# A state-space and mixture-of-experts layer: the last chunk's conv taps behind the softplus's first steps on VectorE, and eps as the bias of the square root

## The chip, the cores and the metric

The kernel runs on one core of a Trainium2 chip. The metric is the device time of the launch in microseconds (us), the median of several runs. The core's engines are named as in the profile: PE is TensorE (matrix multiply) and PEld its weight loads, DVE is VectorE, ACT is ScalarE, POOL is GpSimd, SP is SyncE, which here only issues DMAs. [...]

## The reference

The input is a sequence of 4096 tokens with 256 features. Two layers follow, each with a residual and a layer norm without weights:

```python
xz = input_tensor @ W_in                                  # 256 -> 2 x 512
conv_in, gated = xz[..., :512], xz[..., 512:]
convolved = silu(causal depthwise conv of conv_in, 4 taps, + conv_b)
x_dbl = convolved @ W_x                                   # 512 -> 33
delta = softplus(x_dbl[..., :1]); Bm, Cm = x_dbl[..., 1:17], x_dbl[..., 17:]
h = exp(delta * A) * h + delta * Bm * convolved[..., :16] # scan over the tokens, 16 states
skip_out = sum(h * Cm) + convolved * D_param
x = layernorm(x + (skip_out * silu(gated)) @ W_out)
expert = argmax(x @ Wr.T + br)                            # one of 8 experts for each token
x = layernorm(x + relu(x @ W1[expert] + b1) @ W2[expert] + b2)
```

The layer norm is `(x - m) / sqrt(v + eps)` with eps 1e-5. All is in float32.

## The kernel before, in words

The first layer works through eight blocks of 512 tokens (`TB`), the loop `for k in range(NB)` at L1018. It is pipelined by software: iteration k projects block k, works on the state space of block a = k - 1, on gate, output projection and layer norm of block b = k - 2, and on the routing of block c = k - 3. The second layer runs over 32 blocks of 128 tokens that share an expert (and up to seven that occur seldom, inside `tc.If`, L656); its quarters (`expert()`) are mixed into the last two iterations and fill the time after the loop.

`project(k, c)` (L707) takes one of eight chunks of 128 of the 1024 projected features. Its matmuls are L722. Chunks 0 to 3 are the conv's: ACT copies the result into `xc` (L729) and writes `acc`, the result times the last tap plus the bias (L731); DVE adds the three other taps, each a `scalar_tensor_tensor` over 128x512 (L735). Each tap reads and writes `acc`, so the three are a chain. ACT's silu of chunk c - 2 (L742) is issued in the call of chunk c, behind that chunk's eviction. Chunks 4 to 7 are the gate's: ACT evicts them with a silu (L727). The tiles `acc` have three buffers, the matmul banks `mm` three, the small banks `tr` two.

`gauge(a)` (L750) multiplies the convolved block by `W_x`, and ACT copies the result, `pxs`. `gauge_out(a)` (L764) transposes it (L770); ACT copies it into `parts` (L779); DVE adds the two parts into `xd` (L780). Then comes the softplus of 128x4 values as a series: DVE makes `e` (L785), ACT its exp (L786), DVE ten small steps (L792 to L801), `delta` (L803) and the two writes of `sr` (L804, L807). Meanwhile ACT puts another part into `sr` (L781). `look(k)` multiplies the block by the router's weights, ACT copies that into `rx` (L869), and `look_out(a)` transposes it (`pf`, L876), with `rparts` (L882) behind it. `scan(a)` transposes `sr` (`pt`, L816), takes an exp on ACT (L818), and scans on DVE (L820 to L830) to `hC`. `gate(b)` spreads `hC` by matmul (`py`, L842) and multiplies (L849, L854). `project_out(b, j)` is the output projection (L890) with residual and statistics (L894 to L899); for the last j it takes the square root: DVE adds eps (L904), ACT takes the root (L905), DVE the reciprocal (L906).

The experts' blocks: `hidden` (L581, relu on ACT L590 and on DVE L592), `close` (L606), `finish` with the residual (L629, L631) and the helper `layernorm` (L250): statistics (L254, L256), eps (L258), root (L259), reciprocal (L260), and the row (L261). `scatter` (L645) writes the rows out.

What sets the order: only PE's order is the program's (`tc.manual_schedule(engines={PE})`, L121). The queues of DVE, ACT, POOL and SP are ordered at build time by the framework's scheduler, which takes, of what is ready by its own estimate, what stands first in the program. `tc.issue_after` adds single edges. So `project(k, 3)`, which stands ahead of `gauge_out(a)`, has the higher rank. The part of the loop that the change touches:

Of the kernel before, what the change touches and what calls it, by code (L numbers as in the profile page):

```python
# [37 lines left out]
F32 = mybir.dt.float32  # L38
# [3 lines left out]
AF = mybir.ActivationFunctionType  # L42
ALU = mybir.AluOpType
# [4 lines left out]
P = 128  # L48
T, D = 4096, 256
DI, NS, KC = 512, 16, 4  # L50
NE, FF = 8, 1024
TB = 512
# [4 lines left out]
CC = DI // P  # L57
# [25 lines left out]
EPS = 1e-5  # L83
# [17 lines left out]
def mamba_moe(  # L101
# [17 lines left out]
    nc = tc.nc  # L119

    ctx.enter_context(tc.manual_schedule(engines={mybir.EngineType.PE}))  # L121
    const = ctx.enter_context(tc.tile_pool(name="const", bufs=1))
# [6 lines left out]
    def bank(tag, name, bufs=None):  # L129
        return ps.tile([P, 512], F32, tag=tag, name=name, bufs=bufs)  # L130
# [5 lines left out]
    st = {}  # L136

    def load(i):

        xTb = a2.tile([P, DC, TB], F32, tag="xTb", name=f"xTb{i}")  # L140
        at = slice(i * TB, (i + 1) * TB)
        if i:
            nc.sync.dma_start(xTb, xT[:, at].rearrange("(c p) t -> p c t", p=P))

        xb = a2.tile([P, JT, D + NE], F32, tag="xb", name=f"xb{i}")
        st[i] = {"xTb": xTb, "xb": xb}

    def load_rows(i):
        nc.sync.dma_start(
            st[i]["xb"][:, :, 0:D], x[i * TB : (i + 1) * TB, :].rearrange("(j p) d -> p j d", p=P)  # L150
        )
# [14 lines left out]
    cw = const.tile([P, CC, KC], F32, name="cw")  # L166
# [17 lines left out]
    def load_later():  # L184

        nc.sync.dma_start(wx[:, :, 0:XW], W_x.rearrange("(c p) n -> p c n", p=P))
        nc.sync.dma_start(al, A_log)
        nc.sync.dma_start(dp, D_param)
        nc.sync.dma_start(woutT, W_outT.rearrange("(c p) n -> p c n", p=P))
        nc.sync.dma_start(wout[:, :, 0:D], W_out.rearrange("(c p) d -> p c d", p=P))  # L190
        nc.sync.dma_start(brb, br.to_broadcast([P, NE]))
        nc.sync.dma_start(x1d[T : T + 1, :], lists[0:1, 0:D])

    ident = const.tile([P, P], F32, name="ident")
    make_identity(nc, ident)
    ones = const.tile([P, P], F32, name="ones")
# [53 lines left out]
    def layernorm(pool, rows, done, name):  # L250

        n = rows.shape[0]
        st = pool.tile([P, 6], F32, tag="st", name=f"st{name}")[0:n, :]
        nc.vector.bn_stats(st, rows)  # L254
        mv = pool.tile([P, 2], F32, tag="mv", name=f"mv{name}")[0:n, :]
        nc.vector.bn_aggr(mv, st)  # L256
        sd = pool.tile([P, 1], F32, tag="sd", name=f"sd{name}")[0:n, :]
        nc.vector.tensor_scalar(sd, mv[:, 1:2], EPS, None, ALU.add)  # L258
        nc.scalar.activation(sd, sd, AF.Sqrt)  # L259
        nc.vector.reciprocal(sd, sd)  # L260
        nc.vector.tensor_scalar(done, rows, mv[:, 0:1], sd, ALU.subtract, ALU.mult)  # L261

# [438 lines left out]
    def expert(n=1):  # L701
        for _ in range(n):
            next(quarters)

    def project(i, c):  # L707

        s = st[i]
        xTb = s["xTb"]  # L710
        if c == 0:
            if i == 0:
                s["xc"] = a2.tile([P, CC, KC - 1 + TB], F32, tag="xc", name="xc0")
                nc.gpsimd.memset(s["xc"][:, :, 0 : KC - 1], 0.0)
            s["cv"] = a3.tile([P, CC, TB], F32, tag="cv", name=f"cv{i}")
            s["sg"] = a3.tile([P, CC, TB], F32, tag="sg", name=f"sg{i}")
        xc, cv, sg = s["xc"], s["cv"], s["sg"]
        pm = bank("mm", f"pm{i}_{c}")

        for at in (slice(0, first), slice(first, TB)) if i == c == 0 else (slice(0, TB),):  # L720
            for dc in range(DC):
                nc.tensor.matmul(  # L722
                    pm[:, at], lhsT=win[:, dc, c * P : (c + 1) * P], rhs=xTb[:, dc, at],
                    start=(dc == 0), stop=(dc == DC - 1),
                )
        if c >= CC:
            evicted = nc.scalar.activation(sg[:, c - CC, :], pm, AF.Silu)  # L727
        else:
            nc.scalar.copy(xc[:, c, KC - 1 :], pm)  # L729
            acc = a3.tile([P, TB], F32, tag="acc", name=f"acc{i}_{c}")  # L730
            evicted = nc.scalar.activation(  # L731
                acc, pm, AF.Identity, scale=cw[:, c, KC - 1 : KC], bias=cb[:, c : c + 1]
            )
            for k in range(KC - 1):
                nc.vector.scalar_tensor_tensor(  # L735
                    acc, xc[:, c, k : k + TB], cw[:, c, k : k + 1], acc, ALU.mult, ALU.add
                )
            s["acc", c] = acc
        if ("acc", c - 2) in s:

            with tc.issue_after(evicted.ins):
                nc.scalar.activation(cv[:, c - 2, :], s["acc", c - 2], AF.Silu)  # L742
        if c == CC and i + 1 < NB:

            after = st[i + 1]["xc"] = a2.tile(
                [P, CC, KC - 1 + TB], F32, tag="xc", name=f"xc{i + 1}"
            )
            nc.gpsimd.tensor_copy(after[:, :, 0 : KC - 1], xc[:, :, TB : TB + KC - 1])
# [137 lines left out]
    def project_out(i, j):  # L886
        s_, sg, xb = st[i], st[i]["sg"], st[i]["xb"]
        po = bank("o", f"po{i}_{j}")
        for c in range(CC):
            nc.tensor.matmul(  # L890
                po[:, 0 : D + NE], lhsT=sg[:, c, j * P : (j + 1) * P], rhs=wout[:, c, :],
                start=(c == 0), stop=(c == CC - 1),
            )
        nc.vector.tensor_tensor(xb[:, j, :], po[:, 0 : D + NE], xb[:, j, :], ALU.add)  # L894
        if j == 0:
            s_["mv"] = a2.tile([P, JT, 2], F32, tag="mva", name=f"mva{i}")
        sta = a2.tile([P, 6], F32, tag="sta", name=f"sta{i}_{j}")
        nc.vector.bn_stats(sta, xb[:, j, 0:D])
        nc.vector.bn_aggr(s_["mv"][:, j, :], sta)  # L899
        if j < JT - 1:  # L900
            return
        mv = s_["mv"]
        sd = s_["sd"] = a2.tile([P, JT], F32, tag="sda", name=f"sda{i}")
        nc.vector.tensor_scalar(sd, mv[:, :, 1], EPS, None, ALU.add)  # L904
        nc.scalar.activation(sd, sd, AF.Sqrt)  # L905
        nc.vector.reciprocal(sd, sd)  # L906
        nm = a2.tile([P, JT], F32, tag="nma", name=f"nma{i}")
        nc.vector.scalar_tensor_tensor(nm, mv[:, :, 0], -1.0, sd, ALU.mult, ALU.mult)
        x1 = a2.tile([P, JT, D], F32, tag="x1", name=f"x1{i}", bufs=1)
        for j in range(JT):  # L910
            nc.scalar.activation(
                x1[:, j, :], xb[:, j, 0:D], AF.Identity,
                scale=sd[:, j : j + 1], bias=nm[:, j : j + 1],
            )
        nc.sync.dma_start(
            x1d[i * TB : (i + 1) * TB, :].rearrange("(j p) d -> p j d", p=P), x1
        )
# [94 lines left out]
    def have(i):  # L1012
        return 0 <= i < NB
# [4 lines left out]
    for k in range(NB):  # L1018
        if have(k + 1):
            load(k + 1)  # L1020
        if k == 0:
            load_later()
            load_rows(0)
        if have(k + 1):
            load_rows(k + 1)
        a, b, c = k - 1, k - 2, k - 3

        fill = {NB - 2: (0, 0, 0, 0, 0, 0, 2, 2), NB - 1: (1, 1, 2, 1, 1, 1, 1, 1)}.get(k, (0,) * 8)
        project(k, 0)
        if k == 2:  # L1030
            router_behind(1)
        if have(b):
            gate(b)
        expert(fill[0])
        project(k, 1)
        if have(a):
            gauge(a)
        expert(fill[1])
        project(k, 2)
        if k == 0:  # L1040
            router_weights()
        if have(c - 1):
            tokens_of(c - 1)
        expert(fill[2])
        project(k, 3)
        if have(a):
            gauge_out(a)
        if have(b):
            project_out(b, 0)
        expert(fill[3])  # L1050
        project(k, 4)
        if k == 1:
            router_behind(0)
        if have(c):
            rank(c)
        if have(b):
            project_out(b, 1)
        expert(fill[4])
        project(k, 5)
        if have(c):  # L1060
            blocks_of(c)
        look(k)
        if have(b):
            project_out(b, 2)
        expert(fill[5])
        project(k, 6)
        if have(a):
            look_out(a)
            scan(a)
        if k == NB - 2:  # L1070

            turn(0)
        if have(b):
            project_out(b, 3)
            choose(b)
        expert(fill[6])
        project(k, 7)
        if have(c):
            place(c)
        expert(fill[7])  # L1080
    a, b, c = NB - 1, NB - 2, NB - 3
# [99 lines left out]
```

## Time and profile before

| | |
|---|---|
| time, median of 3 runs | 494.23 us (493.94 to 494.93) |
| profiled execution | 493.76 us, its span 492.1 us |
| granted TensorE clock | 0.991 |
| PE busy | 472.7 us, 96% |
| DVE busy | 346.9 us, 71% |
| ACT busy | 218.8 us, 44% |
| POOL busy | 187.3 us, 38% |
| conv taps, L735 | 96, 71.2 us, mean 771 ns |
| eps adds, L258 and L904 | 32 of 150 ns, 5 of about 142 ns and 8 of 170 ns |
| roots, L259 and L905 | 45, 202 to 206 ns |

A profile line of a group reads: line, engine, operation, out<-in by the program's names, shapes, count, then busy time, mean duration and the idle time of the engine ahead of it with what ended that. A timeline line has start and duration in us, and in brackets the idle time ahead of it. Ends of matmuls are modelled. A part of the time, 1.66 us, lies outside the span. The rows of digits cut the span into 40 slices, each the busy share in tenths.

By stretches of the span: from 50 to 290 us (the loop and what follows of the first layer) PE is busy 237.58 of 240 us and DVE 210.52; from 290 to 440 us PE 149.60 of 150 and DVE 86.45; from 440 us to the end PE 38.52 of 52 and DVE 20.33.

### The profile page before, as it was taken

How to read it: one execution, taken by the hardware profiler on the slowest of the kernel's cores; microseconds unless marked ns; L12 is line 12 of the kernel's file. 1: busy time of each engine (PE TensorE's matmuls, PEld its weight loads, DVE VectorE, ACT ScalarE, POOL GpSimd, SP SyncE). 2: the span in 40 equal slices, each digit the busy share in tenths (PEclk: the TensorE clock that was granted, in tenths of full speed). 3: DMA queues.
4: the chain of work that ended last, by engine and by line, in shares of the span. 5: the costliest groups of instructions: out<-in, count | busy, mean ns of one | idle time of the engine just before them, and what ended most of it. 6: DMA issues, size and time to landing. Idle time of an engine off the chain costs nothing. (4 is left out here: it accounts for less than half of the span.)

```text
span 492.1 us, 7641 instructions
## 1 busy us (share of the span) xinstructions
PE 472.7 (96%) x2602; PEld 353.0 (72%) x2602; DVE 346.9 (71%) x1161; ACT 218.8 (44%) x452; POOL 187.3 (38%) x193
## 2 busy tenths in 40 slices
PE   8999999999999999999999999999999999998893
PEld 5344645555464675777889998999989898987782
DVE  2587979797999889869899788545565655453352
ACT  4786778777878774845342221221212121211120
POOL 2002122444447345233415242444444466542433
PEclk9999999999999999999999999999999999998997
DMA  8401012120308908506666587999871599486500
GB/s 235 156 1 44 0 44 85 45 85 1 128 1 349 361 18 277 191 2 224 218 259 254 214 296 263 375 346 367 325 300 50 202 321 318 143 293 254 194 17 23
DMA packets 23052, 89.59 MB, mean 182 GB/s; under 512 B 4898, under 2 KB 14629, under 8 KB 19298
## 3 DMA queue, kind: packets, MB, share of 16 engines
q0 software_dynamic: 8672, 74.29, 41.3%
q1 hardware_dynamic: 13378, 14.50, 9.1%
q8 instruction: 23, 0.38, 0.3%
q10 hardware_dynamic: 960, 0.27, 0.3%
q14 instruction: 19, 0.16, 0.1%
HBM read 87.35 MB, written 9.54 MB: 197 GB/s over the span
## 5 line engine op out<-in xcount | busy, mean ns | idle before, releaser
L722 PE MATMUL pm<-xTb,win 128*128 128x512 f32 (+1 forms) x260 | 120.6, 595 | 0.5 <-DMA win<-in_W_in 0.5
L581 PEld LDWEIGHTS ph<-xgT,we 128*128 128x128 f32 x864 | 102.2, 194 | 9.7 <-DVEq L656 2.7
L581 PE MATMUL ph<-xgT,we 128*128 128x128 f32 x864 | 104.9, 279 | 3.3 <-DMA out<-long,tidx 2.3
L606 PE MATMUL pe<-we,hT 128*128 128x256 f32 x432 | 99.9, 381 | 0.7 <-DVE hT L592 0.7
L606 PEld LDWEIGHTS pe<-we,hT 128*128 128x128 f32 x432 | 79.5, 190 | 11.7 <-DVE hT L592 1.5
L735 DVE SCALAR_TENSOR_TENSOR acc<-xc,cw,acc 128x512 f32<-128x512 f32 x96 | 71.2, 771 | 15.5 <-ACT acc L731 15.1
L722 PEld LDWEIGHTS pm<-xTb,win 128*128 128x128 f32 x260 | 47.3, 191 | 46.9 <-issue 40.4
L520 POOL DMA_INDIRECT we<-in_experts,widx x32 | 33.8, 1056 | 95.6 <-DVE r L631 32.3
L259 ACT ACTIVATE sdm<-sdm 128x1 f32<-128x1 f32 x32 | 6.5, 202 | 132.8 <-DVE sdm L258 132.7
L890 PE MATMUL po<-wout,sg 128*128 128x264 f32 x256 | 64.1, 392 | 0.0
L854 POOL TENSOR_TENSOR sg<-cv,sg 128x512 f32<-128x512 f32 x22 | 33.9, 1543 | 59.2 <-DVE cv L849 44.3
L890 PEld LDWEIGHTS po<-wout,sg 128*128 128x128 f32 x256 | 46.0, 190 | 10.2 <-issue 2.9
L592 DVE TENSOR_SCALAR hT<-ph,we 128x128 f32<-128x128 f32 x108 | 31.5, 343 | 29.4 <-issue 9.7
L645 POOL DMA_INDIRECT out<-y,tidx x32 | 32.9, 1028 | 42.2 <-DVE y L261 30.0
L503 POOL DMA_INDIRECT xg<-x1d,tidx x32 | 32.3, 1010 | 31.7 <-issue 6.6
L631 DVE TENSOR_TENSOR r<-pe,xs 128x256 f32<-128x256 f32 x32 | 13.5, 422 | 42.3 <-PE pe L606 38.5
L590 ACT ACTIVATE hT<-ph,we 128x128 f32<-128x128 f32 x108 | 30.8, 366 | 26.5 <-PE ph L581 18.3
L979 POOL TENSOR_SCALAR rowh<-lrow,row,code 128x256 f16<-128x256 bf16 x20 | 25.8, 1299 | 26.8 <-DVE row L971 26.8
L849 DVE SCALAR_TENSOR_TENSOR cv<-cv,dp,py 128x256 f32<-128x256 f32 x64 | 28.9, 470 | 2.4 <-PE py L842 2.4
L727 ACT ACTIVATE sg<-pm 128x512 f32<-128x512 f32 x32 | 19.0, 595 | 17.1 <-PE pm L722 14.8
L581 PE MATMUL ph<-wide,we 128*128 128x160 f32 (+1 forms) x160 | 24.4, 310 | 2.3 <-DVEq L656 2.3
L581 PEld LDWEIGHTS ph<-wide,we 128*128 128x128 f32 x160 | 23.8, 190 | 2.9 <-DVEq L656 2.7
(221 smaller groups left out, 612.3 us busy)
## 6 DMA issues: line engine op xcount, KB each, us to landing
xb<-in_x SPq DMA_DIRECT2D x8, 512.0 KB, 4.8
x1d<-x SPq DMA_DIRECT2D x8, 512.0 KB, 5.4
xTb<-in_xT SPq DMA_DIRECT2D x7, 512.0 KB, 3.5
win<-in_W_in SPq DMA_DIRECT2D x1, 512.0 KB
we<-in_W_outT SPq DMA_DIRECT2D x1, 512.0 KB
wout<-in_W_out SPq DMA_DIRECT2D x1, 512.0 KB
we<-in_experts,widx POOLq DMA_INDIRECT x32
xg<-x1d,tidx POOLq DMA_INDIRECT x32
```

The source lines that it names most:

```text
L503: nc.gpsimd.indirect_dma_start(out=to, out_offset=None, in_=x1d[0:rows, :], in_offset=bass.IndirectOffsetOnAxis(ap=at, axis=0),)
L520: nc.gpsimd.indirect_dma_start(out=wes[n][:, :], out_offset=None, in_=experts, in_offset=bass.IndirectOffsetOnAxis(ap=weights[n], axis=0), ...
L581: nc.tensor.matmul(ph[:, n * w : (n + 1) * w], lhsT=we[:, at : at + P], rhs=xgT[:, dc * w : (dc + 1) * w], start=(dc == 0), stop=(dc == DC ...
L590: nc.scalar.activation(hT[:, fc, :], ph[:, n * w : (n + 1) * w], AF.Relu, bias=bias)
L592: last[b] = nc.vector.tensor_scalar(hT[:, fc, :], ph[:, n * w : (n + 1) * w], bias, 0.0, ALU.add, ALU.max)
L606: nc.tensor.matmul(py[:, 0:D], lhsT=hT[:, fc, 0:P], rhs=out_weights(fc), start=(fc == 0), stop=(fc == FC - 1),)
L645: moved = nc.gpsimd.indirect_dma_start(out=out, out_offset=bass.IndirectOffsetOnAxis(ap=at, axis=0), in_=rows, in_offset=None, bounds_chec ...
L722: nc.tensor.matmul(pm[:, at], lhsT=win[:, dc, c * P : (c + 1) * P], rhs=xTb[:, dc, at], start=(dc == 0), stop=(dc == DC - 1),)
L735: nc.vector.scalar_tensor_tensor(acc, xc[:, c, k : k + TB], cw[:, c, k : k + 1], acc, ALU.mult, ALU.add)
L849: nc.vector.scalar_tensor_tensor(cv[:, c, at], cv[:, c, at], dp[:, c : c + 1], py[:, 0 : TB // 2], ALU.mult, ALU.add,)
L854: eng.tensor_tensor(sg[:, c, :], cv[:, c, :], sg[:, c, :], ALU.mult)
L890: nc.tensor.matmul(po[:, 0 : D + NE], lhsT=sg[:, c, j * P : (j + 1) * P], rhs=wout[:, c, :], start=(c == 0), stop=(c == CC - 1),)
```

## The change

The three taps of a chunk become a helper `taps(i, c)`. `project` calls it for chunks 0 to 2 as before. For chunk 3 the loop calls it after `gauge_out(a)` and before `project_out(b, 0)`. So the sum of the gauge's parts (L780) and the softplus's steps now have the higher rank on DVE, and the last chunk's taps the lower. The adds of eps on DVE are gone at both places; a 128x1 tile with eps, set once on POOL, is the bias of ACT's square root, which now reads the variance itself. The number of taps and roots is the same.

```diff
+    eps = const.tile([P, 1], F32, name="eps")
+    nc.gpsimd.memset(eps, EPS)
     ident = const.tile([P, P], F32, name="ident")
...
-        nc.vector.tensor_scalar(sd, mv[:, 1:2], EPS, None, ALU.add)
-        nc.scalar.activation(sd, sd, AF.Sqrt)
+        nc.scalar.activation(sd, mv[:, 1:2], AF.Sqrt, bias=eps[0:n, :])
...
+    def taps(i, c):
+        acc, xc = st[i]["acc", c], st[i]["xc"]
+        for k in range(KC - 1):
+            nc.vector.scalar_tensor_tensor(
+                acc, xc[:, c, k : k + TB], cw[:, c, k : k + 1], acc, ALU.mult, ALU.add
+            )
...
-            for k in range(KC - 1):
-                nc.vector.scalar_tensor_tensor(
-                    acc, xc[:, c, k : k + TB], cw[:, c, k : k + 1], acc, ALU.mult, ALU.add
-                )
             s["acc", c] = acc
+            if c < CC - 1:
+                taps(i, c)
...
-        nc.vector.tensor_scalar(sd, mv[:, :, 1], EPS, None, ALU.add)
-        nc.scalar.activation(sd, sd, AF.Sqrt)
+        nc.scalar.activation(sd, mv[:, :, 1], AF.Sqrt, bias=eps)
...
         project(k, 3)
         if have(a):
             gauge_out(a)
+
+        taps(k, CC - 1)
         if have(b):
             project_out(b, 0)
```

## The prediction

> **What bounds the kernel now.** I read the first two parts of the page, then TensorE's own waits, then the timeline around the longest of them, then the timeline of the end.
>
> ```profile
> span 492.1 us, 7641 instructions
> PE 472.7 (96%) x2602; PEld 353.0 (72%) x2602; DVE 346.9 (71%) x1161; ACT 218.8 (44%) x452; POOL 187.3 (38%) x193
> PE   8999999999999999999999999999999999998893
> DVE  2587979797999889869899788545565655453352
> ```
>
> TensorE (PE) is the wall: it is thin only at the start and in the last tenth. VectorE (DVE) is nearly full in the chunk phase, up to about 290 us, and half idle later. So an edit on DVE or ScalarE (ACT) pays only where PE waits for it. Those places, from PE's waits:
>
> ```profile
> PE ph L581 <- DMA out<-long,tidx: 2.3, 1, 2.3
> PE ph L581 <- DVEq L656: 2.3, 1, 2.3
> ...
> PE pt L816 <- DVE mva L899: 1.4, 2, 0.7
> ...
> PE pt L816 <- ACT rx L869: 0.7, 1, 0.7
> PE ph L581 <- DVE y L261: 0.6, 1, 0.6
> ```
>
> The columns are total us, times, longest. Two families: `pt` (L816), the transposes of `sr`, which `gauge_out` ends with (L807), and `ph` (L581), the first expert matmul behind an If (L656). One `pt` wait, iteration k = 3, on the timeline:
>
> ```profile
> 79.47 4.05 DVE L735 SCALAR_TENSOR_TENSOR acc<-xc,cw,acc 128x512 f32<-128x512 f32 x6
> ...
> 81.44 0.36 ACT L779 COPY parts<-pxo 128x264 f32<-128x264 f32 x1
> ...
> 83.44 0.28 DVE L780 TENSOR_TENSOR xd<-parts 128x132 f32<-128x132 f32 x1
> 83.65 0.74 DVE L735 SCALAR_TENSOR_TENSOR acc<-xc,cw,acc 128x512 f32<-128x512 f32 x1
> ...
> 85.32 0.21 ACT L786 ACTIVATE e<-e 128x4 f32<-128x4 f32 x1
> ...
> 89.18 0.38 PE L876 MATMUL pf<-ident,rx 128*128 128x128 f32 x2
> ...
> 89.77 0.34 DVE L807 TENSOR_TENSOR sr<-xd,sr 128x64 f32<-128x64 f32 x1
> ...
> 90.26 0.61 PE L816 MATMUL pt<-ident,sr 128*80 128x128 f32 x4 [0.70 <-DVE mva L899]
> ```
>
> `parts` is there at 81.80, but `xd` starts at 83.44, because taps of chunks 2 and 3 go first; everything to `sr` (90.11) hangs on it. The page names L899, but in k = 3, 4 and 5 `pt` starts exactly 0.147 us after L807 ends, so L807 is the releaser. Start to start the transposes of a group are 0.109 us apart, and in k = 2, where nothing is late, `pt` follows `pf` by 0.109 too. With that yardstick PE loses 0.83 (k = 1), 0.86 (k = 3), 0.86 (k = 4) and 0.31 (k = 5): **2.86 us**. (The listed idle, 0.66 + 0.70 + 0.70 + 0.15, is shorter as it counts from a modelled end.) In k = 1 the last to come is not `sr` (37.48) but ACT's `rx` copy (37.79), which stands behind the exp and its table loads in ACT's queue. In k = 6 and 7 and behind the loop `sr` is early.
>
> The end, one If at 445 us:
>
> ```profile
> 443.80 0.18 DVE L256 BATCH_NORM_AGGREGATE mvm<-stm 128x2 f32<-128x6 f32 x1
> 444.01 0.15 DVE L258 TENSOR_SCALAR sdm<-mvm 128x1 f32<-128x1 f32 x1
> 444.20 0.20 ACT L259 ACTIVATE sdm<-sdm 128x1 f32<-128x1 f32 x1 [5.30 <-DVE sdm L258]
> ```
>
> PE is idle during this chain and restarts when DVE has passed the If.
>
> [...] loads last 1283 ns, and L731, with two pointers, takes 783 ns where the copy of the same tile (L729) takes 580, so about 102 each. [...] here exp stands between silus and pays a load each way (84.02 and 85.54 in k = 3). [...]
>
> **The change part by part.** The order in which PE works is written by hand; the other queues are ordered by the framework, with program order as rank, so an instruction of lower rank slips into a gap of a chain of higher rank.
>
> *Taps of chunk 3 moved behind `gauge_out`.* Nothing is added: three L735 (0.68 us apart back to back, 0.74 alone) change places in each of 8 iterations. They go past `gauge_out`'s DVE work (L780 to L807) and its ACT steps L779, L781, L786; no DMA, SP or POOL work is passed. As long as the taps of two chunks are in the queue they fill each other's gaps, and `xd` comes only at the last tap. With chunk 3 ranked behind, `xd` can go as soon as `parts` is there and a chunk 2 tap has ended: about 82.2 in k = 3 instead of 83.44, and more in k = 4, where 107.75 stands against 110.94. So `e` and the exp come 1.2 us or more earlier. From the end of `xd` to that of the exp, with its load, it is 1.8 us (83.72 to 85.53), and the chunk 3 taps (2.0 us) fill just this time, which other DVE work fills now (84.46 to 86.15). That other work then falls among the twelve small steps L792 to L807. DVE is 10.66 of 10.90 us busy from 79.4 to 90.3, so `sr` comes earlier only by what now stands in front of it and then stands behind. At least L894 and L898 at 88.96 and 89.44, which need a late matmul, should be: about 0.7 us. If more of the second projection's work falls behind, up to 1.7. Needed is 0.86. I take 0.70 each in k = 3 and 4, all 0.31 in k = 5 (its `xd` now waits from 135.23 to 138.41), and in k = 1, where the exp and with it `rx` come 0.8 earlier, 0.60 of 0.83. Sum 0.70 + 0.70 + 0.31 + 0.60 = **2.3 us**; bounds 0 and 2.86. What is late next is `py` (L842), which waits for `hC`; its chain starts from L894 of the last projection, which follows PE itself, so it moves along. DVE idles 2.32 us at 90.4, so work pushed behind `sr` has room.
>
> *The silu of chunk 3* waits for these taps: their last ends at 84.39, the silu starts at 87.33 (2.9 us of cover), then `rx` (87.85 to 88.21) has 0.8 us to `pf`. Costed at nothing; without that cover each us is a us of PE per iteration.
>
> *Sqrt with eps as bias.* 37 L258 and 8 L904 go, about 0.15 us each, 6.7 us of DVE time; each sqrt gets a pointer, 0.2 to about 0.3 us. In a waiting chain 0.19 (444.01 to 444.20) goes and 0.1 comes: 0.09 saved. It counts where PE or the end waits: the Ifs at 445, 457 and 469 us and the last block (485.34 to the end), 4 x 0.09 = **0.37 us**. Bounds: 0 if the bias fetch eats it all, 0.76 if it is free. Elsewhere ACT waits for this add (133 us listed) but nobody waits for ACT. Behind the sqrt in ACT's queue stand the next block's relus, 0.1 later at worst, and all of PE's waits for `hT` are 0.7 us.
>
> *eps memset*: one 128x1 memset on POOL ahead of the identity, 0.1 us by the constants' rows. PE's warm-up shifts, but its first real matmul waits 0.47 us for the DMA at 4.91. Nothing; 0.1 if that cover were gone.
>
> Sum: 2.3 + 0.37 = 2.7 us; I take 0.2 off because all queues are ordered anew and small waits (0.3 us at 172, 175 and 234) can grow. The profiled execution took 493.76 (span 492.1 and 1.66 around it), which gives 491.3; the median of the runs is 494.23, 0.47 higher, which gives **491.7**.
>
> **The rivals.** *Nothing at PE*: all DVE work in front of `sr` stays in front, as small work fills every gap of the twelve steps, and only the end's 0.37 is left: 493.8. For it: DVE's saturation up to 90.3. Against: L894 and L898 can't come before their matmul, and `sr` now stands behind them.
>
> *Slower*: the chunk 3 taps fall behind the softplus chain, and their silu blocks ACT in front of `rx`. It decides from a last tap later than about 88.1 (84.39 + 2.9 + 0.8). If the taps followed `sr`, they would end near 89.6, 1.5 us too late in each of k = 1 to 5: +7.5 - 2.5 = +5, so 499.2. Against: the taps still outrank the projection's and the rank work, and the exp's 1.8 us is free for them.
>
> **How the numbers follow.** Forecast 0.60, nothing 0.27, slower 0.13. A measurement of this kernel tells about 0.2% (0.99 us) from no change. A few of the second case end below 493.24: faster 0.62, same 0.25, slower 0.13. The range runs from 490.9 (2.86 + 0.5) to 494.9 (the second case with 0.7 us of new waits); it leaves out the slower case and little else.
>
> **What would show it.** Right: `xd` within 1 us of `parts` in k = 3 to 5, L786 a us earlier relative to L779, the `pt` waits gone or under 0.2, the sqrts near 295 ns, the span down by about 2.5 before 180 us and 0.3 behind 440. Wrong: `pt` still waiting on L807, a silu of chunk 3 with idle time in front of it on ACT, or a new PE wait at `py` or `pf` that takes the place.

## The result, and the profile after

| | before | after |
|---|---|---|
| median, first comparison (7 runs each) | 494.23 us | 490.78 us |
| ratio, 95% interval | | 0.9919 [0.9898, 0.994] |
| second comparison (67 and 22 runs) | 495.77 us | 493.80 us, 0.9966 [0.9949, 0.9984] |
| third comparison (34 and 18 runs) | 493.52 us | 491.32 us, 0.9957 [0.9936, 0.9978] |
| profiled execution, its span | 493.76, 492.1 us | 490.78, 489.1 us |

Faster, as forecast, and the first measured time, 490.78 us, lies 0.12 us below the range's low end of 490.9. The two later comparisons give 1.7 and 2.1 us (494 us times 0.0034 and 0.0043), less than the 2.5 us forecast. Both have to be explained: what the change itself is worth, and what the first comparison had on top.

The page of the kernel after: its head, the busy line and two rows of tenths.

```profile
span 489.1 us, 7602 instructions
PE 472.0 (97%) x2602; PEld 353.9 (72%) x2602; DVE 340.1 (70%) x1116; ACT 224.1 (46%) x453; POOL 185.2 (38%) x194
PE   8999999999999999999999999999999999998893
DVE  2587969798999988869889788545555555453352
```

DVE lost 45 instructions and 6.8 us (346.9 to 340.1). ACT gained 5.3 us: 45 roots by about 0.1 us are 4.2, and there is one more table load (49 in place of 48, 1.28 us each). As forecast, neither of these is the gain. PE's own waits after (total us, times, longest):

```profile
PE pt L822 <- ACT rx L875: 0.7, 1, 0.7
...
PE prx L869 <- DVE rk L969: 0.4, 1, 0.4
```

The two `pt` waits put down to `mva` are gone. The one of k = 1 is as it was. A new one has come: `prx`, the router's matmul, waits for `rk`. Iteration k = 3 on the timeline after:

```profile
81.00 0.38 ACT L785 COPY parts<-pxo 128x264 f32<-128x264 f32 x1
...
82.74 0.28 DVE L786 TENSOR_TENSOR xd<-parts 128x132 f32<-128x132 f32 x1
82.95 0.73 DVE L711 SCALAR_TENSOR_TENSOR acc<-xc,cw,acc 128x512 f32<-128x512 f32 x1
...
83.70 0.62 ACT L748 ACTIVATE cv<-acc 128x512 f32<-128x512 f32 x1
...
84.34 1.28 ACT L792 ACT_TABLE_LOAD   x1
...
85.63 0.20 ACT L792 ACTIVATE e<-e 128x4 f32<-128x4 f32 x1
...
85.87 0.17 DVE L798 TENSOR_SCALAR s<-e 128x4 f32<-128x4 f32 x1
...
89.57 0.24 DVE L813 TENSOR_TENSOR sr<-xd,sr 128x64 f32<-128x64 f32 x1
...
89.96 0.61 PE L822 MATMUL pt<-ident,sr 128*80 128x128 f32 x4
```

`xd` starts 1.36 us after `parts` ends (1.64 before), and all three taps of chunk 3 stand behind it, where it was one. At this place the kernel after runs 0.47 us later (a DMA at the start), so `xd` is at 82.27 on the clock of before: 82.2 was forecast. `sr` ends at 89.81 and `pt` starts with no bracket: the wait is gone.

The way there is not the same in every iteration. In k = 3 the exp (85.63, on the clock of before 85.16) comes only 0.16 us earlier than the 85.32 of before, because a silu stands ahead of its table load on ACT. The gain comes behind it: `s` (L798) starts 0.03 us after the exp has ended, where other work on DVE held it up for 0.62 us before:

```profile
84.02 1.28 ACT L786 ACT_TABLE_LOAD   x1
...
86.15 0.15 DVE L792 TENSOR_SCALAR s<-e 128x4 f32<-128x4 f32 x1
```

So `sr` ends 0.77 us earlier. In k = 4 it goes as forecast. First before, then after, which is 0.31 us ahead at this place:

```profile
107.37 0.38 ACT L779 COPY parts<-pxo 128x264 f32<-128x264 f32 x1
...
110.94 0.28 DVE L780 TENSOR_TENSOR xd<-parts 128x132 f32<-128x132 f32 x1
...
112.81 0.21 ACT L786 ACTIVATE e<-e 128x4 f32<-128x4 f32 x1
```

```profile
107.07 0.38 ACT L785 COPY parts<-pxo 128x264 f32<-128x264 f32 x1
...
108.64 0.28 DVE L786 TENSOR_TENSOR xd<-parts 128x132 f32<-128x132 f32 x1
...
111.02 0.20 ACT L792 ACTIVATE e<-e 128x4 f32<-128x4 f32 x1
```

With the 0.31 us taken off, the exp is 1.5 us earlier and `sr` 1.3 us (117.60 before, 116.03 after).

**A sum over all pairs of matmuls.** PE's 2602 matmuls have the same order in every kernel here. For each neighbouring pair I took the time from start to start in each of thirteen profiles, and what it is above the shortest of them. A wait that all thirteen have, such as that of `pt` in k = 1, doesn't show in this. Added up by place, in us (before in two executions, after in three):

| place | before | before again | after | after again | after, third |
|---|---|---|---|---|---|
| `pt`, k = 3 | 0.81 | 0.80 | 0.03 | 0.02 | 0.00 |
| `pt`, k = 4 | 0.86 | 0.86 | 0.00 | 0.00 | 0.00 |
| `pt`, k = 5 | 0.31 | 0.30 | 0.00 | 0.00 | 0.00 |
| `prx`, k = 5 | 0.02 | 0.02 | 0.48 | 0.48 | 0.49 |
| `ph` at 297 us | 0.29 | 0.28 | 0.00 | 0.00 | 0.00 |
| `ph` behind the Ifs, 443 and 455 us | 0.20 | 0.20 | 0.07 | 0.07 | 0.07 |
| **what follows the kernel** | **2.49** | **2.46** | **0.58** | **0.57** | **0.56** |
| start, up to 12 us | 1.29 | 1.59 | 1.72 | 3.77 | 1.86 |
| `po` behind a stretched `oh`, k = 4 to 6 | 0.0 | 0.0 | 0.0 | 1.73 | 0.78 |
| `pe` waiting for `hT`, 412 and 472 us | 1.27 | 1.29 | 0.00 | 1.25 | 0.00 |
| half clock, 440 to 452 us | 1.66 | 1.66 | 1.66 | 1.66 | 0.04 |

The upper part is the same to 0.03 us in every execution of a kernel: **1.9 us is the change's own** at these places. The lower part changes between executions of the same program; its rows add up to 2.7 to 8.4 us. In the two first profiles it was 1.27 (`hT`) in favour of after and 0.43 (start) against. Small waits at 171 to 174 us are in neither part: 0.70 twice before, 0.40, 0.57 and 0.57 after.

Two things remain open. A stretched `oh` (a small step of DVE, see the last section) was seen ahead of `po` in two of the three profiles of after and in none of the two of before. It meets POOL's product at the same point in both kernels (0.60 us into it), but with so few profiles it isn't shown that the change leaves this row alone. And the granted clock was higher for after: its mean was 0.9930 beside 0.9920 in the second comparison and 0.9936 beside 0.9914 in the third. One stretch of half clock is 1.66 us of time and 0.0034 of that mean. My estimate from these numbers is that at equal clock the mean times (2.1 and 2.5 us apart) differ by 1.6 and 1.4 us, a little under the 1.9.

### The profile page after: what moved, and what is told of

The parts are those of the page before. It is cut to its first block, busy times and chain, and to the rows that moved or that the text cites. A ratio compares the mean times of both kernels' runs of the same rounds, so it can differ in the third digit from the quotient of the medians.

```text
span 489.1 us, 7602 instructions
## 1 busy us (share of the span) xinstructions
PE 472.0 (97%) x2602; PEld 353.9 (72%) x2602; DVE 340.1 (70%) x1116; ACT 224.1 (46%) x453; POOL 185.2 (38%) x194
## 5 line engine op out<-in xcount | busy, mean ns | idle before, releaser
L711 DVE SCALAR_TENSOR_TENSOR acc<-xc,cw,acc 128x512 f32<-128x512 f32 x96 | 72.7, 777 | 16.0 <-ACT acc L739 15.6
L260 ACT ACTIVATE sdm<-mvm,eps 128x1 f32<-128x1 f32 x32 | 9.4, 295 | 144.2 <-DVE mvm L258 138.4
L860 POOL TENSOR_TENSOR sg<-cv,sg 128x512 f32<-128x512 f32 x22 | 32.8, 1495 | 59.4 <-DVE cv L855 45.9
L737 ACT COPY xc<-pm 128x512 f32<-128x512 f32 x32 | 18.6, 581 | 18.1 <-PE pm L730 17.8
```

The source lines that it names most:

```text
L711: nc.vector.scalar_tensor_tensor(acc, xc[:, c, k : k + TB], cw[:, c, k : k + 1], acc, ALU.mult, ALU.add)
L860: eng.tensor_tensor(sg[:, c, :], cv[:, c, :], sg[:, c, :], ALU.mult)
```

## Experiments

Each kernel computes the whole reference. Ratios are against the kernel before on the same chip: the first four ran on one chip, the next four on another, the last three on a third. The edits of the first two are shown against the kernel before, the later ones against the kernel after.

**The taps alone** (the diff's `taps`, without the bias).

```diff
             s["acc", c] = acc
+            if c < CC - 1:
+                taps(i, c)
...
+        taps(k, CC - 1)
```

> Only the three taps of chunk 3 are moved behind the gauge; the adds of eps on VectorE and the roots are as before. Theory (the gain is the pt waits of the loop): pt waits of k = 3, 4 and 5 are gone (1.9 to 2.0 us by starts of matmuls), the one of k = 1 stays at 0.83, and a new wait of about 0.45 us at prx in k = 5 comes, as rank's first step stands further back on VectorE: net 1.5 us faster than before, about 492.7. Rival (half of the gain is the shorter layer norm of the experts): at most 1.0 us faster than before, and the rest comes with the eps edit alone.

Measured: 493.80 us, 0.9969 [0.9948, 0.9989], so 1.5 us. The `pt` waits of k = 4 and 5 are gone, that of k = 3 is 0.17 in the sum, `prx` has its 0.48, `pt` of k = 1 is unchanged. By the sum: 0.64 + 0.86 + 0.31 - 0.46 = 1.35. The interval of the time, 0.5 to 2.6 us, leaves room for the rival's 1.0; it is the sum that puts the gain at these places. Its profile also had two stretched `oh`, 1.72 us.

**The bias alone** (the same at L904, and the tile `eps` as in the change).

```diff
-        nc.vector.tensor_scalar(sd, mv[:, 1:2], EPS, None, ALU.add)
-        nc.scalar.activation(sd, sd, AF.Sqrt)
+        nc.scalar.activation(sd, mv[:, 1:2], AF.Sqrt, bias=eps[0:n, :])
```

> Only the adds of eps are gone and eps is the bias of the root; the taps stand where they stood. Theory: the layer norm chain of an expert block is 0.09 us shorter, of which 0.07 are lost again where VectorE's aggregate now waits for ScalarE's reading of the variance: 0.1 to 0.2 us at the Ifs and the end in all. By the build's order of the queues the k = 3 iteration also gets another order (chunk 3's taps further back), so the pt wait of k = 3 may shrink by up to 0.8 us and that of k = 4 stays at 0.86: 0.2 to 1.0 us faster, about 493.6. Rival: the edit frees VectorE in the expert phase and takes away the waits of the hidden matmuls' evictions at 414 and 475 us (1.06 us) that the profile of before had: 1.5 us faster or more.

Measured: 494.68 us, 0.9992 [0.9969, 1.0016]. By the time alone this is no change. By the sum of pairs it has the 0.29 at 297 us and 0.13 behind the Ifs, which the taps alone have not; and `pt` of k = 3 fell to 0.29 because DVE's queue was ordered anew there; those of k = 4 and 5 stayed (0.84, 0.31). Its profile also had the stretched `oh` in three iterations, 2.7 us, which no part of the edit asks for.

**The kernel before, again.**

> The kernel before, unchanged, for a second profile. Theory: the waits of pe for hT at 414 and 475 us (0.55 and 0.51 us by starts) belong to that one execution, in which TensorE's semaphore updates came late and in bunches; they are not at these places in this profile, and the pt waits of k = 1, 3, 4 and 5 are all there with the same sizes. Rival: they belong to the program, and are at 414 and 475 us again. Time within 0.1% of the runs of before.

Measured: 496.17 us, 1.0008 [0.9988, 1.0027]. All four `pt` waits are back, and both `hT` waits at the same places in the program. So the `hT` waits are no accident of one execution, as I had thought; the later groups show that they are no part of the program either.

**The kernel after, again.**

> The changed kernel, unchanged, for a second profile on this chip. Theory: no pt wait in k = 3 to 5, pt of k = 1 at 0.83 us and prx of k = 5 at about 0.45 us again; late bunches of TensorE's semaphore updates may come at other places. Time 3 to 3.5 us below before (0.7%).

Measured: 493.80 us, 0.9966 [0.9949, 0.9984]. So 1.7 us, not the 3 to 3.5 expected. The `pt` waits are gone as in the first profile; `hT` (1.25) and two stretched `oh` (1.73) are there, which the first did not have. The profiled execution took 496.02 us against 490.78 for the same program, and its rows of the lower part add up to 8.4 us against 3.4.

**The taps behind `rank`.**

```diff
-        taps(k, CC - 1)
         if have(b):
             project_out(b, 0)
...
         if have(c):
             rank(c)
+        taps(k, CC - 1)
```

> The changed kernel with the last chunk's taps called two places later in the loop, behind rank(c). Theory (rank's rk was pushed behind the moved taps on DVE, and it frees the bank that prx needs in k = 5): rk is early again, the prx wait of 0.41 us in k = 5 is gone, the pt waits of k = 3 to 5 stay gone, and the silu of chunk 3 still has its cover; by the trace 0.4 us less than the changed kernel, ratio to before 0.995 to 0.997. Rival (the prx wait belongs to the bank's other user, or to the softplus chain that now runs at the same time): it stays at 0.3 to 0.5 us. Second rival (the taps come too late for their silu): ACT idles in front of the silu of chunk 3 in k = 3 to 5, rx is late, and pf or pt waits 0.3 us or more.

Measured: 492.01 us, 0.994 [0.9918, 0.9962]. First `rk` (DVE) and `prx` (PE) of k = 5 in the kernel after, then in this one:

```profile
139.08 0.15 DVE L969 TENSOR_TENSOR rk<-pr,oh 128x32 f32<-128x32 f32 x1
...
139.28 0.64 PE L869 MATMUL prx<-xTb,wr 128*32 128x256 f32 x8 [0.41 <-DVE rk L969]
```

```profile
136.67 0.17 DVE L969 TENSOR_TENSOR rk<-pr,oh 128x32 f32<-128x32 f32 x1
...
138.86 0.64 PE L869 MATMUL prx<-xTb,wr 128*32 128x256 f32 x8
```

`rk` comes 2.4 us earlier and the bracket is gone: the theory holds. The matmul banks `tr` are two, taken in turn, and in k = 5 a table's `pn` (at 138.70 us in after) takes the one between, so that `prx` gets the bank of `pr`, which `rk` frees. In return the taps fall among the softplus steps, and `pt` waits 0.26 in k = 4 and 0.14 in k = 3: a gain of 0.48 at one place and 0.37 back.

**`rx` of k = 1 on DVE.**

```diff
-        nc.scalar.copy(st[i]["rx"], prx[:, 0:n])
+        (nc.vector.tensor_copy if i == 1 else nc.scalar.copy)(st[i]["rx"], prx[:, 0:n])
```

> The changed kernel with the copy rx of iteration 1 alone on DVE and not on ACT. Theory (in k = 1 pt waits for ACT's rx, which stands behind the exp and its two table loads in ACT's queue, and not for sr): the pt wait of k = 1, 0.67 to 0.83 us in every profile so far, falls under 0.3, and the span loses about 0.5 us; whatever is left of the wait is sr. Rival (sr is as late as rx, or DVE reaches rx later than ACT did): the wait stays above 0.5. Nothing else moves; ratio to before 0.995 to 0.997.

Measured: 491.56 us, 0.9928 [0.9902, 0.9953]. In its profile, end of the softplus on DVE and then PE:

```profile
38.18 0.23 DVE L813 TENSOR_TENSOR sr<-xd,sr 128x64 f32<-128x64 f32 x1
...
38.55 0.60 PE L822 MATMUL pt<-ident,sr 128*80 128x128 f32 x4 [0.89 <-DVE sr L813]
```

`pt` doesn't read this `rx`: it takes the bank of `prx`, which the copy frees. The expected gain did not come. With `rx` out of ACT's queue the wait grew by 0.23, because the copy stood in front of the softplus on DVE and `sr` came at 38.41, not 37.95. In the kernel after `sr` ends 0.3 us before `rx` (37.95 and 38.26), so even an `rx` that cost DVE nothing would win no more than about that. Whether it would is not shown, as this edit moved `sr` too. The later waits for `py` (0.46 in the sum) went, so the net is a gain of 0.24.

**The taps later still**, behind `project_out(b, 1)`: a test of the slower rival.

```diff
         if have(b):
             project_out(b, 1)
+        taps(k, CC - 1)
```

> The changed kernel with the last chunk's taps called behind project_out(b, 1). It tests the slower rival of the prediction: the silu of chunk 3 stands in front of rx in ACT's queue, so taps that end more than about 3.7 us later than before hold up rx, and pf and pt with it. Theory (the cover is as costed, and here the last tap falls behind the first softplus steps): ACT idles 1 to 2 us in front of the silu of chunk 3 in k = 3 to 5, and PE waits 0.3 to 1.5 us in each of them at pf, pt or prx; 1 to 4 us slower than the changed kernel, ratio to before 0.998 to 1.005. Rival (the cover is larger than the timeline showed, or pt waits for sr in any case): no new wait of PE above 0.3 in k = 3 to 5, ratio as the changed kernel's.

Measured: 492.37 us, 0.9932 [0.9901, 0.9963], no slower than the kernel after in its comparisons, where 0.998 to 1.005 was expected. Iteration k = 4: ACT, then DVE and PE.

```profile
115.45 0.36 ACT L875 COPY rx<-prx 128x256 f32<-128x256 f32 x1
116.39 0.63 ACT L748 ACTIVATE cv<-acc 128x512 f32<-128x512 f32 x1 [0.58 <-DVE acc L711]
...
118.81 0.61 PE L822 MATMUL pt<-ident,sr 128*80 128x128 f32 x4 [0.16 <-DVE sr L813]
```

The taps do come late for their silu, which waits 0.58 us, but `rx` now runs ahead of it: the scheduler orders ACT's queue too, and put the late silu behind `rx`. So the mechanism that my slower rival named did not act here; it needs `rx` to stand behind the silu. What PE waits for is `sr` (0.33 and 0.40 in k = 4 and 3), as taps stand among the softplus steps. The price of moving too far is that, 0.8 us with k = 5, of which 0.48 comes back as `rk` is early; not 5.

**The gate's first product on DVE.**

```diff
-            eng = nc.vector if c == CC - 1 or (c % 2 and i >= NB - 2) else nc.gpsimd
+            eng = nc.vector if c in (0, CC - 1) or (c % 2 and i >= NB - 2) else nc.gpsimd
```

> The changed kernel with the gate's product of chunk 0 on DVE and not on POOL (7 or 8 instructions change the engine). In some executions the one-hot oh on DVE takes 1.2 to 1.3 us in place of 0.18 when it runs beside POOL's product, the last product is then late and PE waits 0.95 us at po. Theory (it is the meeting with POOL's first product that stretches oh): with no POOL product at that time every oh takes under 0.25 us, the po waits of 0.9 us don't occur, and the cost is about 0.6 us of DVE time for each product, which may show as a pt wait or none. Rival (oh is stretched by something else, or the next product on POOL takes the place): some oh are still above 1 us. In time 0.993 to 0.999 of before.

Measured: 494.94 us, 0.9995 [0.998, 1.001]. Every `oh` ahead of the `po` of k = 4 to 6 is at 0.18 us. That fits the theory, but three such in one profile could be chance; stronger is that in the other profiles each of the nine stretched ones ends 0.05 us behind POOL's product. And `oh` of k = 3 now meets a product and took 0.78 us. The rival's second half came true: in k = 4 to 6 the small step `earlier` (L947, 0.15 us where it is free) took 0.95 us beside the product that POOL now does first. `po` waits 0.88 in k = 4 and 5, 0.57 in k = 3, 0.71 in k = 6. All that the change had gained is gone.

**The kernel after, a third time.**

> The changed kernel a third time, on another occasion. Theory (the change's own part is about 1.9 us: 0.79, 0.86 and 0.31 at pt, less 0.46 at prx in k = 5, plus 0.29 at 297 us and 0.1 at the Ifs; what the first comparison showed above this belongs to executions, with waits for hT and half clock after pauses): ratio 0.995 to 0.9975 of before, and the profile has the same waits at pt, prx and the Ifs as the first, whatever its clock does. Rival (the first comparison's 0.992 is the change's value, and something in the other session took half of it): ratio 0.990 to 0.994.

Measured: 491.32 us, 0.9957 [0.9936, 0.9978], in the theory's range; about 1 us of it is the clock, by the estimate above. The last column of the table above is its profile: the same upper part, no `hT` waits, one stretched `oh`, full clock at 440 us.

**Rank first, `rx` on DVE, four buffers for `mv`.**

```diff
-        mv = pool.tile([P, 2], F32, tag="mv", name=f"mv{name}")[0:n, :]
+        mv = pool.tile([P, 2], F32, tag="mv", name=f"mv{name}", bufs=4)[0:n, :]
```

(with the two edits above)

> The changed kernel with the taps behind rank(c), rx of iteration 1 on DVE, and four buffers for the statistics mv of layernorm. Theory (each step takes away its own wait): no prx wait in k = 5, the py waits of k = 1 gone and pt there at 0.9, pt of k = 3 and 4 under 0.3, and the aggregate in layernorm follows the statistics in 34 ns at all places; 0.3 to 0.5 us less than the changed kernel by the trace, ratio to before 0.994 to 0.9965. Rival (the queues, ordered anew, put other waits in): the sum of PE's waits between 36 and 165 us is not below the changed kernel's.

Measured: 490.09 us, 0.9905 [0.987, 0.994]. By the sum of pairs `prx` and `py` lost 0.48 each, and `pt` got 0.22, 0.11 and 0.24 back: 0.39 less than after between 36 and 165 us, without the stretched `oh` of its profile (0.77). Its ratio is the lowest of all here, but of its lead on the kernel after only these 0.4 us, and 0.1 to 0.2 behind 450 us, are shown: its few runs (6) had a mean granted clock of 0.9938 beside 0.9914 for the kernel before, and one clock step of 1.66 us is 0.0034 of the span.

**Four buffers alone.**

> The changed kernel with four buffers for layernorm's statistics mv in place of two, everything else the same. Theory (ACT's root now reads mv itself, so the next aggregate but one must wait for ACT before it writes the buffer, which costs the 70 ns between 34 and 103 seen at four places): with four buffers the gap is 34 ns at every place, no semaphore instruction stands in front of the aggregates on DVE, and the waits at the Ifs of 445 and 457 us are about 0.07 us shorter. Rival (the gap has another reason): 103 ns stay. In time nothing that can be measured, 0.994 to 0.998 of before.

Measured: 491.79 us, 0.994 [0.9917, 0.9962]. One If's chain after (statistics, aggregate, root), and the aggregate with four buffers:

```profile
453.14 0.43 DVE L256 BATCH_NORM_STATS2 stm<-r 128x6 f32<-128x256 f32 x1
453.67 0.18 DVE L258 BATCH_NORM_AGGREGATE mvm<-stm 128x2 f32<-128x6 f32 x1
453.88 0.29 ACT L260 ACTIVATE sdm<-mvm,eps 128x1 f32<-128x1 f32 x1 [6.92 <-DVE mvm L258]
```

```profile
452.86 0.43 DVE L256 BATCH_NORM_STATS2 stm<-r 128x6 f32<-128x256 f32 x1
453.33 0.18 DVE L258 BATCH_NORM_AGGREGATE mvm<-stm 128x2 f32<-128x6 f32 x1
```

Between the statistics' end and the aggregate there were 103 ns, and now 35. The trace of after has four semaphore instructions in front of aggregates (453.6 to 482.1 us), and of this kernel none. The If wait at 455 us fell by 0.07, the tail by 0.06. So the edit that took an add out of the chain had put a wait in: ACT's root now reads `mv` itself, and the next but one aggregate, which writes the same buffer, must wait for ACT.

## Why the prediction was right and wrong

- **The mechanism** (the softplus chain behind the taps holds up `pt` in k = 3 to 5) was right: 0.78 + 0.86 + 0.31 = 1.95 us came, where 0.70 + 0.70 + 0.31 was written. Of these waits only 0.05 to 0.08 in k = 3 was left, so what I had held back for small work in front of `sr` was too much. Two of its details were wrong. `xd` still starts 1.2 to 1.4 us after `parts`, not within 1 us. And in k = 3 the exp is not 1.2 us earlier but 0.16, and of the two steps that were to fall behind `sr` only one did (L904 at 89.73; L900 at 89.23 still stands ahead). That `sr` was in time there came from the gap behind the exp, which I had not counted: in part luck.
- **The step that failed by its reason** is "in k = 1, where the exp and with it `rx` come 0.8 earlier, 0.60 of 0.83". Nothing came. DVE's order around `xd` is the same before and after in k = 1: `xd` starts 0.43 us after `parts` (32.28 after 31.85) and 0.44 (32.76 after 32.32), so there was nothing to move. There is no gate or projection of block b on DVE yet, which is the likely reason. I carried over a picture from k = 3 without reading k = 1's own rows.
- **A misread line:** I gave `rx` 0.8 us "to `pf`". But `pf` transposes the `rx` of the block before. In k = 1 of the kernel before it starts ahead of the copy, and it is `pt`, in the bank of `prx`, that follows:

```profile
36.84 0.38 PE L876 MATMUL pf<-ident,rx 128*128 128x128 f32 x2
...
37.43 0.36 ACT L869 COPY rx<-prx 128x256 f32<-128x256 f32 x1
...
37.89 0.61 PE L816 MATMUL pt<-ident,sr 128*80 128x128 f32 x4 [0.66 <-ACT rx L869]
```

In k = 3 the cover was thus 1.2 us (88.21 to 89.40, two steps of 0.11 behind the start of `pf`). The forecast's sum doesn't hang on it; the slower rival's limit of 88.1 does, and would be 88.5.

- **Tail and Ifs, 0.37:** the forecast's 0.09 in each chain was right (root 202 to 295 ns, so 93 more with the bias; aggregate to `y` 1.24 to 1.15), but 0.07 of it was paid back at four places by the wait for `mv`. The sum of pairs has 0.13 at the Ifs and a tail longer by 0.03 (8.27 to 8.30).
- **Not foreseen, for:** 0.29 at 297 us. It goes with the bias alone and stays with the taps alone. There DVE works off the small steps of a table in front of `xgT`; that one add less in this queue brings `xgT` forward is argued, not tested. I had listed small waits only as something that can grow.
- **Not foreseen, against:** 0.46 at `prx`. I wrote that work pushed behind "has room", and named the second projection's steps; but `rk` is among what is pushed, and it frees a bank. The question that I left out is what each delayed instruction releases.
- **The sum:** 2.5 us forecast, 1.9 by the trace, 1.7 and 2.1 in the two larger comparisons (1.6 and 1.4 at equal clock). The terms' errors (+0.24 for `pt`, -0.60 for k = 1, -0.27 for the tail and Ifs, +0.29, -0.46, and +0.20 for what I took off at the end) add up to -0.60.
- **The range** is the step by which the first measured time was missed. Its low end, 2.86 + 0.5 us, took only the change's own bounds, and put what differs between executions at nothing. Seven runs of a kernel whose executions differ by 1.66 us per clock step and 1.3 us with `hT` don't give the change to 0.5 us. The change's own 1.9 leaves 1.5 of the first comparison's 3.45 us. The `hT` waits, 1.27 us in the profile of before and none in that of after, have the size for most of it; but one profile on each side can't tell what the other runs had, and it stays open.
- **Rivals:** "nothing at PE" was wrong at PE, and the slower one did not come even with the late taps above. A late silu held in front of `rx` was not tested.

## What to carry to other kernels

When low-ranked work is pushed back in a queue to let a chain through, list for every pushed instruction the buffer it frees and who waits for that, and look at each iteration's own order before multiplying one iteration's gain. When an operation begins to read a tile that it did not read before, count the tile's buffers: here the root's new read of `mv` put 0.07 us in front of the aggregate (103 ns, and 35 with four buffers). Judge an edit of some tenths of a per cent by start-to-start times at its places in several executions; the median of a few runs measures the execution's lottery as well.

## What the runs showed of the hardware

**Half clock by chance.** The stretch from 46 to 48 us in the kernel after (with one at 444), and in the kernel with the late taps; the third number from the end is the granted clock.

```profile
46.00:48.00 2.00, 2.00 (x10) 0.48 (x8) 2.00 (x4) 1.27 (x2) 0.99 (x2) 1.00 0.00 0
444.00:446.00 2.00, 2.00 (x12) 2.00 (x11) 0.00 (x0) 0.18 (x1) 1.66 (x2) 0.50 0.61 136
```

```profile
46.00:48.00 2.00, 2.00 (x6) 0.36 (x6) 2.00 (x3) 0.86 (x2) 0.98 (x2) 0.50 0.00 0
```

At some places the clock halves or doesn't, for 3.41 us in the profiles of before and after (from 445.70 and 443.66 us), and costs 1.66 us each time: there matmuls of 128x128 start 0.21 us apart in place of 0.11. It came behind 440 us in nine of thirteen profiles, at 46 and 457 us in two. Behind 440 us and at 457 us it follows PE's wait of about 2.3 us at an If (it begins 0.54 us after the wait's end in before, 0.91 in after); at 46 us no such wait is near: in the ten us ahead PE was busy for 9.15 us. What brings the step at either kind of place, and why it comes in some executions only, no run here shows.

**A small DVE step stretched beside POOL's product, or not.** `oh` (128x32) beside POOL's product, and PE behind it, in the second execution of after:

```profile
131.51 1.85 POOL L860 TENSOR_TENSOR sg<-cv,sg 128x512 f32<-128x512 f32 x1 [1.29 <-DVE cv L855]
132.11 1.30 DVE L944 TENSOR_TENSOR oh<-back,best 128x32 bf16<-128x32 f32 x1
...
135.71 0.71 PE L896 MATMUL po<-wout,sg 128*128 128x264 f32 x2 [0.96 <-DVE sg L860]
```

In the first execution the same two, again 0.60 us apart, took 1.91 and 0.18 us:

```profile
129.47 1.91 POOL L860 TENSOR_TENSOR sg<-cv,sg 128x512 f32<-128x512 f32 x1 [1.28 <-DVE cv L855]
130.07 0.18 DVE L944 TENSOR_TENSOR oh<-back,best 128x32 bf16<-128x32 f32 x1
```

The 1.30 us end 0.05 us behind the product, the 0.18 us lie in the middle of one; what makes the difference is not shown. Which of the two happens is not set by the program here: the same code had it ahead of none, two and one of the `po` of k = 4 to 6, and of the 36 such meetings in twelve profiles, all 0.60 us into the product, nine were stretched. A later `oh` (at 260 us), which starts 0.12 us into its product, was stretched to 1.2 us in all twelve.

**Late signals from PE.** Where `hT` was late, in the first profile of before and in the first eight experiments, PE's semaphore updates had come late and in bunches about 43 ns apart (in before six from 474.72 to 474.93 us; in after they are 0.43 us apart at this place), and DVE started 1.6 to 2.0 us after the matmuls' end. In the other four profiles it was 0.04 and 0.25 us. The two waits sum to 1.2 to 1.4 us in all four profiles of the first chip, 0.88 to 0.94 in the four of the next, and none in the three of the third, whatever the kernel. What decides is open.
